# Expert blocks of a routed layer: the last 26 blocks with their three PE steps interleaved over three blocks, and separate places for the two weights

## Chip, core and metric

The kernel runs on one core of a Trainium2 chip. The metric is the device time of one launch in microseconds; times before are the median of three runs. One further execution was recorded by the profiler, and all engine times below come from it.

## What is computed

The reference is one layer over 6250 nodes with 256 features, all in float32:

```python
xn = layernorm(x)
x  = x + gnn(xn, edges) + linear_attention(xn)      # 100000 edges, sorted by target
z  = layernorm(x)
gate = z @ gate_w + gate_b                          # 16 experts, top 2 of them, softmax weights
h    = relu(z @ w1[e] + b1[e])                      # 256 -> 512
y    = h @ w2[e] + b2[e]                            # 512 -> 256
out  = x + layernorm(z + sum_over_top2(weight * y)) * gamma + beta
```

A graph part, a linear attention part and a mixture of experts follow each other for each node; the routing of a node can be computed as soon as its own row is done.

## The kernel before

Nodes are cut into 49 tiles of 128 rows. The host lays out one row of `experts` per expert and partition: the first product's weights (`WA` = 1024 floats), then the second product's weights with both biases (1284 floats). `WROW` is their sum.

Everything from the edge stage on is written as small Python generators that a `Weave` runs. A generator is added with a slot number, does a step, and yields how many slots later its next step comes; steps of one slot run in the order in which their generators were added. A slot is no time. It only fixes the order in which instructions are recorded, and so the order within each engine's queue and within SP's queue of DMA issues. Each engine then works through its own list in order and waits where data or a buffer isn't ready.

The stages in slot order:

- Edge stage: 782 chunks of 128 edges. For each, POOL gathers 128 rows (L1181), DVE builds a selection matrix (L1185), and PE multiplies six slots later (L1194). One chunk per slot.
- `residual(...)` finishes the rows of two tiles; `route(...)` assigns the tokens of a phase of tiles to slots of expert blocks of 128 tokens; `scatter(...)` sends the tokens to `xslots` (L931). `PHASES` lists the phase ends 8, 12, ..., 40, 46, 49. The last phase has `flush` true: it also closes all half filled blocks.
- `expert(n, j, ...)` is one block, 114 in all. With `s` its first slot and gaps (5, 4): at `s` SP issues the load of the first weights (called w1 here) and of the block's tokens x; at `s+5` the load of the second weights and both biases (w2); at `s+9` PE transposes x (`xtp`, L995) and ACT copies the result (L999); at `s+11` PE does the first product (`hp`, L1005) and ACT adds the bias and applies relu (L1010); at `s+13` PE does the second product (`yp`, L1014) and DVE adds the bias (L1018); at `s+15` SP issues the store to `yslots`. All DMA issues of a block go through the helper at L959. Blocks of phases up to the ninth start 7 slots apart, later ones 4 slots apart. Blocks 88 to 113 belong to the last phase.
- `combine(ts_, ...)` finishes a pair of tiles: POOL gathers the two expert rows of each token (L1044), ACT prepares the row (L1052), DVE adds the weighted rows (L1059), takes the statistics (L315, L316), gets the inverse deviation through ACT's square root (L321, L322) and normalises (L1067, L1068, L1070), then SP stores the output. The pairs of tiles 0 to 35 (`CUT` = 36) need only blocks up to number 84 and are added 5 slots apart beside the last blocks; the pairs of tiles 36 to 48 are added from 18 slots after the last block's start, and their gathers wait for the stores of all blocks.

Buffers are handed out by `Places`: `take()` gives the first free place in a list, `give()` puts it back at the end. A place made of tiles of `Q` can be taken only when those tiles have been read by the stage that wrote them. `homes["w"]` has four places of `WROW` floats: two in the tile `early` and two of ten tiles of `Q` each (14 to 23, 24 to 33). `x` has three places, `xT`, `hT` and `y` have two each, `got` (what combine gathers) has fourteen. The PSUM results of a block, `xtp`, `hp` and `yp`, come from one pool of six banks.

If the token counts were unusual, a second version behind a branch (L1214) would do all blocks again; with these inputs it is not run.

Of the kernel before, what the change touches and what calls it, by code (L numbers as in the profile page):

```python
# [31 lines left out]
P = 128  # L32
N = 6250
D = 256
# [17 lines left out]
FJ = F // P  # L52
KB = (2 * N + NE * (BLK - 1)) // BLK
WROW = 2 * F + FJ * D + FJ + D
# [72 lines left out]
WA = 2 * F  # L127
# [112 lines left out]
def windowed_layer(ctx: ExitStack, tc: tile.TileContext, X, rows3, ident, loc_t, w_t, W, b, gamma, beta, wqT, wkvT, wprojT, bproj,  # L240
# [6 lines left out]
    def bcast(ap, n):  # L247
        return bass.AP(tensor=ap.tensor, offset=ap.offset, ap=[[0, P], [1, n]])
# [88 lines left out]
    early = wp.tile([P, 2 * WROW], F32, name="early")  # L337
# [178 lines left out]
    def bank(name):  # L516
        return ps.tile([P, 512], F32, name=name, tag="bank")
# [440 lines left out]
    def sync(to, source):  # L958
        issued[0] = nc.sync.dma_start(to, source).ins  # L959
        return issued[0]  # L960

    stores = {}

    def expert(n, j, homes, bank, gap):

        def row(i):
            if not loaded.get(i):
                _, regs = nc.values_load_multi_w_load_instructions(
                    s["rows"][0:1, i, j:min(j // 8 * 8 + 8, ends[j])], engines=[mybir.EngineType.SP],
                    min_val=0, max_val=(MOST if i == 0 else NE - 1) * P,  # L970
                    skip_runtime_bounds_check_because="bounded by a minimum where it is computed")
                loaded[i] = list(regs)
            return loaded[i].pop(0)

        at, slots = row(1), row(0)
        wp_ = homes["w"].take()
        w = wp_()[:, :WROW]
        sync(w[:, :WA], experts[bass.ds(at, P), :WA])
        xp = homes["x"].take()
        xs = xp()  # L980
        i = sync(xs, xslots[bass.ds(slots, P), :])
        if n is not None:
            for m in range(n + 1, len(PHASES)):
                tc.declare_no_dep(i, group=f"tokens_{m}", reason="a full block takes no more tokens")
            tc.add_to_no_dep_group("loads", i)
        yield gap[0]
        sync(w[:, WA:], experts[bass.ds(at, P), WA:])
        w1 = w[:, :WA].rearrange("p (c f) -> p c f", c=2)
        w2 = w[:, WA:WA + FJ * D].rearrange("p (j d) -> p j d", j=FJ)
        b1 = w[:, WA + FJ * D:WA + FJ * D + FJ]  # L990
        b2 = w[:, WROW - D:]
        yield gap[1]
        tp = bank("xtp").rearrange("p (k c) -> p k c", k=4)
        for c in range(2):
            nc.tensor.transpose(tp[:, c, :], xs[:, c * P:(c + 1) * P], ident)  # L995
        homes["x"].give(xp)
        xTp = homes["xT"].take()
        xT = xTp().rearrange("p (k c) -> p k c", k=2)
        nc.scalar.copy(xT, tp[:, :2, :])  # L999
        yield 2  # L1000

        hp = bank("hp").rearrange("p (f c) -> p f c", f=FJ)
        for f in range(FJ):
            for c in range(2):
                nc.tensor.matmul(hp[:, f, :], w1[:, c, f * P:(f + 1) * P], xT[:, c, :], start=(c == 0), stop=(c == 1))  # L1005
        homes["xT"].give(xTp)
        hTp = homes["hT"].take()
        hT = hTp().rearrange("p (k c) -> p k c", k=FJ)
        for f in range(FJ):
            act(hT[:, f, :], hp[:, f, :], AF.Relu, bias=b1[:, f:f + 1], scale=1.0)  # L1010
        yield 2
        yp = bank("yp")
        for f in range(FJ):
            nc.tensor.matmul(yp[:, :D], hT[:, f, :], w2[:, f, :], start=(f == 0), stop=(f == FJ - 1))  # L1014
        homes["hT"].give(hTp)
        y_ = homes["y"].take()
        y = y_()
        v.tensor_add(y, yp[:, :D], b2)  # L1018
        homes["w"].give(wp_)
        yield 2  # L1020
        before_it = issued[0]
        i = sync(yslots[bass.ds(slots, P), :], y)
        if n is not None:
            tc.declare_no_dep(i, group="stores", reason="every block has rows of its own", keep=[before_it])
            tc.add_to_no_dep_group("stores", i)
            stores[j] = i
            if j >= FIRST:
                tc.declare_no_dep(i, group="gathers", reason="later blocks hold no token of the first tiles")
                tc.add_to_no_dep_group("late", i)
        homes["y"].give(y_)  # L1030
# [67 lines left out]
    def spare(t, n=1):  # L1098
        return range(t, t + n), lambda: Q[:, t:t + n, :].rearrange("p t c -> p (t c)")

    homes = {"token": Places(*[spare(t) for t in range(4)]),
             "x": Places(*[spare(t) for t in (4, 5, 6)]),
             "xT": Places(spare(7), spare(8)),
             "hT": Places(*[((), lambda j=j: hTs[j]) for j in range(2)]),
             "y": Places(spare(13), spare(34)),
             "w": Places(((), lambda: early[:, :WROW]), ((), lambda: early[:, WROW:]), spare(14, 10), spare(24, 10)),
             "got": Places(*[spare(t) for t in range(35, NT)])}


    weave = Weave()  # L1110
    PRE = 14
    at = -PRE
# [3 lines left out]
    at = int(at) + 6  # L1116
# [11 lines left out]
    block, ends, scattered = 0, {}, 0  # L1128
    a = lo = 0
    for n, b in enumerate(PHASES):  # L1130
        flush = b == NT
        for t0 in range(a, b, 2):
            t1 = min(b, t0 + 2)
            at = max(at, min(NCH, 16 * t1 + 4) + LAG + 3)
            weave.add(at, residual(range(t0, t1)))
            last_at = at
            for t in range(t0, t1):
                summed_at[t] = at + 3
                if t + RING < NT and t >= 4:
                    sum_from(t + RING)  # L1140
            at += 10
        hi = USUAL if flush else 2 * b - (9 if n < AFTER else -1 if n == AFTER else 4)
        ready = max(last_at + RES, scattered - 2)
        weave.add(ready, route(a, b, lo, hi, n == 0, n == AFTER, flush))
        if flush or n == AFTER:
            weave.add(ready + 6, token_weights(*((CUT, NT) if flush else (0, CUT))))
        slow = 0 if flush else 1
        weave.add(ready + 2, scatter(n, a, b, 9, "token" if slow else "got", slow))
        scattered = ready + 11 + 2 * (b - a) * slow
        ready += 14 + (2 * (b - a) * slow)  # L1150
        for j in range(lo, hi):
            ends[j] = hi
            block = max(block + (7 if n <= AFTER else 4), ready)
            weave.add(block, expert(n, j, homes, bank, (4, 3) if n < 3 else (5, 4)))
            if j == FIRST - 1:
                ready_a = block + 18
        lo, a = hi, b
# [7 lines left out]
    at = max(ready_a, last_at + RES)  # L1165
    for t0 in range(0, NT, 2):
        if t0 == CUT:
            at = max(at, block + 18)
        weave.add(at, combine(range(t0, min(NT, t0 + 2)), homes, mp, last))
        at += 5  # L1170
    hrow = rows3.rearrange("p a (i d) -> p (a i) d", d=D)
# [3 lines left out]
    while slot < NCH + LAG or weave.steps:  # L1175
        for t in range(NT * (slot + PRE) // PRE, NT * (slot + PRE + 1) // PRE if slot < 0 else 0):
            table(t)
        c = slot
# [8 lines left out]
        c = slot - LAG  # L1187
# [26 lines left out]
    with tc.If(again), ExitStack() as tail:  # L1214
        tail.enter_context(by_hand(tc))
        mp = tail.enter_context(tc.tile_pool(name="w_again", bufs=2))
        ps = tail.enter_context(tc.tile_pool(name="w_again_ps", bufs=8, space=bass.MemoryType.PSUM))
        last = mp.tile([P, 2, D], F32, name="last", bufs=1)
        nc.sync.dma_start(last[:, 0, :], bcast(f_gamma, D))
        nc.sync.dma_start(last[:, 1, :], bcast(f_beta, D))  # L1220

        def places(n, size, name):
            tiles = [mp.tile([P, size], F32, name=f"{name}{j}", bufs=1) for j in range(n)]
            return Places(*[((), lambda t=t: t) for t in tiles])

        homes = {"x": places(4, D, "x"), "xT": places(2, D, "xT"), "hT": places(2, F, "hT"),
                 "y": places(2, D, "y"), "w": places(4, WROW, "w"), "got": places(8, D, "got")}
        weave = Weave()
        block = 0
        loaded.clear()  # L1230
        stores.clear()
        row = bank("row")
        nc.tensor.matmul(row[0:1, :P], s["code"], ident, start=True, stop=True)
        listed(row, 0, MOST, True)
        for j in range(MOST):
            ends[j] = MOST
            weave.add(block, expert(None, j, homes, bank, (5, 4)))
            block += 4
        block += 18
        for t0 in range(0, NT, 2):  # L1240
            weave.add(block, combine(range(t0, min(NT, t0 + 2)), homes, mp, last))
            block += 6
        slot = 0
        while weave.steps:
            weave.run(slot)
            slot += 1
# [485 lines left out]
```

## Time and profile before

| what | value |
|---|---|
| three runs, us | 1525.33, 1528.05, 1530.75 (median 1528.05) |
| profiled execution: its own time, us | 1528.39 |
| profiled execution: span of the trace, us | 1526.6 |
| granted TensorE clock, mean over the span | 0.941 |
| edge chunks' last products | about 1226 us from the start of the span |
| scatter of the last phase's tokens | 1279 to 1288 us |
| last 26 blocks, first product of the first to last add | 1320.3 to 1463.7 us |
| loads of the first and of the second weights | 114 of 512 KB, 114 of 642 KB |

The profile's lines give a start time in microseconds from the start of the span, a duration, the engine, the line of the kernel, the operation, "output <- inputs", shapes and a count of merged instructions. In square brackets stands the engine's idle time just ahead and what ended it. One float32 matmul is two recorded instructions. In tables by stretch the columns are PE, PEld (weight load), DVE, ACT and POOL busy microseconds with instruction counts, then granted clock, DMA share and GB/s.

### The profile page before, as it was taken

Reading aid. Unit: us, or ns where it says so; the run is one execution under the profiler, and the core shown is the slowest. Engines: PE = TensorE matmul, PEld = TensorE weight load, DVE = VectorE, ACT = ScalarE, POOL = GpSimd, SP = SyncE. Lnnn points to the kernel's source line nnn. Section 1 sums busy time; section 2 is a strip of 40 time slices with the busy share of each in tenths; the row PEclk is TensorE's granted clock in tenths of the full one; section 3 lists DMA queues with packets and bytes.
Section 4 is the critical chain, followed back from the end, with each engine's and each line's share of the span. In section 5 each row is a group of like instructions: output and inputs, shape, how many; then the busy total and the mean of one; then the engine's idle time right before and its main releaser. Section 6 shows DMA issues by size and latency. Waiting matters only on the chain.

```text
span 1526.6 us, 24293 instructions
## 1 busy us (share of the span) xinstructions
PE 1252.2 (82%) x6930; PEld 981.7 (64%) x6930; DVE 921.1 (60%) x3262; ACT 509.3 (33%) x1353; POOL 967.0 (63%) x999
## 2 busy tenths in 40 slices
PE   4869999988867989898898998979899887877720
PEld 3836666666645768677776776767778766666620
DVE  8753444468875655657457574665655653388845
ACT  3653444433231323233233232322323243444320
POOL 1017777777777777777777777777777631565142
PEclk9999999999878989899999999999999999999975
DMA  9889933333337768778677877876778757899942
GB/s 274 273 257 379 376 107 101 103 98 114 102 114 236 231 218 276 244 260 279 221 260 242 272 266 227 277 238 227 242 274 265 251 185 275 310 376 378 327 128 69
DMA packets 176557, 357.04 MB, mean 234 GB/s; under 512 B 26643, under 2 KB 115656, under 8 KB 176406
## 3 DMA queue, kind: packets, MB, share of 16 engines
q1 hardware_dynamic: 128458, 226.32, 42.9%
q0 software_dynamic: 47712, 128.17, 26.9%
q8 instruction: 62, 1.02, 0.3%
q10 hardware_dynamic: 236, 0.80, 0.2%
q14 instruction: 89, 0.73, 0.2%
HBM read 280.82 MB, written 74.36 MB: 233 GB/s over the span
## 4 chain that ended last, share of the span: by engine, by line
PE 39%; DVE 19%; DMA 15%; issue 5%; ACT 3%; POOL 2%; SPq 0%; ACTq 0%; POOLq 0%; DVEq 0%
PE acc L1194 12%; DMA rows<-w_hs,src_t 9%; PE yp L1014 9%; PE hp L1005 7%; DMA w_xslots<-Q,slot_i 3%; PE hp L671 2%; DVE xn L1059 2%; DVE hot L1185 2%; PE kq L553 2%; DVE bnst L315 2%; PE mix L687 2%; DMA Q<-in_experts 1%; DMA early<-in_experts 1%; POOL w_xslots L931 1%; PE gl L714 1%
## 5 line engine op out<-in xcount | busy, mean ns | idle before, releaser
L1181 POOL DMA_INDIRECT rows<-w_hs,src_t x782 | 758.1, 969 | 333.0 <-issue 100.0
L1194 PE MATMUL acc<-rows,hot 128*128 128x256 f32 x1564 | 446.2, 401 | 73.4 <-DMA rows<-w_hs,src_t 61.3
L1194 PEld LDWEIGHTS acc<-rows,hot 128*128 128x128 f32 x1564 | 276.2, 197 | 149.4 <-issue 61.3
L1185 DVE TENSOR_SCALAR hot<-iota_g,loc_t,w_t 128x128 f32<-128x128 f32 x782 | 247.1, 359 | 14.5 <-PE acc L1194 13.7
L1044 POOL DMA_INDIRECT Q<-w_yslots,slot_i x98 | 99.8, 1019 | 113.4 <-DMA w_yslots<-Q 64.4
L1005 PE MATMUL hp<-Q,early 128*128 128x128 f32 x1136 | 143.8, 281 | 12.5 <-ACT Q L999 12.2
L1005 PEld LDWEIGHTS hp<-Q,early 128*128 128x128 f32 x1136 | 139.6, 196 | 21.4 <-ACT Q L999 18.4
L931 POOL DMA_INDIRECT w_xslots<-Q,slot_i x98 | 103.2, 1053 | 75.6 <-issue 66.8
L1014 PE MATMUL yp<-early,hT 128*128 128x256 f32 x568 | 140.1, 390 | 12.8 <-ACT hT L1010 12.8
L1010 ACT ACTIVATE hT<-hp,early 128x128 f32<-128x128 f32 x284 | 81.1, 368 | 146.5 <-PE hp L1005 103.9
L1014 PEld LDWEIGHTS yp<-early,hT 128*128 128x128 f32 x568 | 107.8, 193 | 32.8 <-ACT hT L1010 18.4
L999 ACT COPY Q<-xtp 128x256 f32<-128x256 f32 x114 | 42.1, 370 | 249.1 <-PE xtp L995 239.6
L1203 DVE SCALAR_TENSOR_TENSOR agg<-acc,dinv,agg 64x256 f32<-64x256 f32 x135 | 65.2, 483 | 72.5 <-PE acc L1194 68.5
L1018 DVE TENSOR_TENSOR Q<-yp,early 128x256 f32<-128x256 f32 x71 | 30.1, 424 | 122.6 <-PE yp L1014 122.6
L553 PE MATMUL kq<-early,xnT 128*128 128x512 f32 (+1 forms) x196 | 98.1, 624 | 4.4 <-ACT xnT L549 4.4
L559 DVE SCALAR_TENSOR_TENSOR row<-two_a,two_b 128x256 f32<-128x256 f32 (+1 forms) x49 | 21.0, 429 | 131.6 <-ACT two_b L557 131.6
L1005 PE MATMUL hp<-Q 128*128 128x128 f32 x688 | 88.2, 283 | 12.8 <-ACT Q L999 12.8
L1005 PEld LDWEIGHTS hp<-Q 128*128 128x128 f32 x688 | 84.0, 196 | 19.0 <-ACT Q L999 17.8
L1014 PE MATMUL yp<-Q,hT 128*128 128x256 f32 x344 | 85.2, 391 | 13.2 <-ACT hT L1010 13.2
L1010 ACT ACTIVATE hT<-hp,Q 128x128 f32<-128x128 f32 x172 | 49.1, 368 | 99.0 <-PE hp L1005 53.8
L1014 PEld LDWEIGHTS yp<-Q,hT 128*128 128x128 f32 x344 | 64.7, 193 | 25.8 <-ACT hT L1010 17.6
L321 ACT ACTIVATE sd<-mv,eps_t 128x2 f32<-128x2 f32 (+2 forms) x76 | 22.8, 300 | 152.7 <-DVE mv L316 148.7
(272 smaller groups left out, 1774.2 us busy)
## 6 DMA issues: line engine op xcount, KB each, us to landing
early<-in_experts SPq DMA_DIRECT2D x71, 642.0 KB
early<-in_experts SPq DMA_DIRECT2D x71, 512.0 KB
Q<-in_experts SPq DMA_DIRECT2D x43, 642.0 KB
Q<-in_experts SPq DMA_DIRECT2D x43, 512.0 KB
w_xslots<-zero_b SPq DMA_DIRECT2D x16, 1024.0 KB
w_yslots<-zero_b SPq DMA_DIRECT2D x16, 1024.0 KB
Q<-w_xslots SPq DMA_DIRECT2D x114, 128.0 KB
w_yslots<-Q SPq DMA_DIRECT2D x114, 128.0 KB
```

Source lines behind the costliest of these rows:

```text
L315: v.bn_stats(st[:r], src_tile)
L553: nc.tensor.matmul(kq[:r], xnT[:, k, :r], wkq[:, k, :], start=(k == 0), stop=(k == 1))
L931: i = nc.gpsimd.indirect_dma_start(out=xslots, out_offset=IndirectOffsetOnAxis(ap=slot_i[:r, t, k:k + 1], axis=0), in_=y[:r], in_offset=No ...
L999: nc.scalar.copy(xT, tp[:, :2, :])
L1005: nc.tensor.matmul(hp[:, f, :], w1[:, c, f * P:(f + 1) * P], xT[:, c, :], start=(c == 0), stop=(c == 1))
L1010: act(hT[:, f, :], hp[:, f, :], AF.Relu, bias=b1[:, f:f + 1], scale=1.0)
L1014: nc.tensor.matmul(yp[:, :D], hT[:, f, :], w2[:, f, :], start=(f == 0), stop=(f == FJ - 1))
L1044: g = nc.gpsimd.indirect_dma_start(out=got[i, k]()[:r], out_offset=None, in_=yslots, in_offset=IndirectOffsetOnAxis(ap=slot_i[:r, t, k:k + ...
L1181: nc.gpsimd.indirect_dma_start(out=hrows[c], out_offset=None, in_=hs, in_offset=IndirectOffsetOnAxis(ap=src_t[:, c:c + 1], axis=0))
L1185: v.tensor_scalar(hots[c], iota_g[:, group_of(c) % 2, :], loc_t[:, c:c + 1], w_t[:, c:c + 1], op0=OP.is_equal, op1=OP.mult)
L1194: nc.tensor.matmul(accs[g], hots.pop(c), hrows.pop(c), start=begin, stop=end)
L1203: v.scalar_tensor_tensor(agg(t)[p0:p1], acc[p0:p1, :], dinv[p0:p1, t:t + 1], agg(t)[p0:p1], op0=OP.mult, op1=OP.add)
```

## The change

`expert` gets a parameter `apart`, the slots from the transposes to the first product and from the first to the second. It is 5 for the blocks of the last phase and 2 for all others, as before. The steps of a last-phase block then lie at `s+9`, `s+14`, `s+19` and the store at `s+21`. The weights are taken as two buffers: `w1` at `s`, given back after the first product, and `w2` at `s+5`, given back after the bias add. `w1` has two places in `early` and two of four tiles of `Q`; `w2` has two in `early` and two of six tiles of `Q`. The pairs of tiles from 36 on are added from 24 slots after the last block's start. The branch that is not run is adapted.

```diff
-    def expert(n, j, homes, bank, gap):
+    def expert(n, j, homes, bank, gap, apart):
...
-        wp_ = homes["w"].take()
-        w = wp_()[:, :WROW]
-        sync(w[:, :WA], experts[bass.ds(at, P), :WA])
+        w1p = homes["w1"].take()
+        w1 = w1p()
+        sync(w1, experts[bass.ds(at, P), :WA])
+        w1 = w1.rearrange("p (c f) -> p c f", c=2)
...
         yield gap[0]
-        sync(w[:, WA:], experts[bass.ds(at, P), WA:])
...
+        w2p = homes["w2"].take()
+        w = w2p()[:, :WROW - WA]
+        sync(w, experts[bass.ds(at, P), WA:])
...
         nc.scalar.copy(xT, tp[:, :2, :])
-        yield 2
+        yield apart
...
         homes["xT"].give(xTp)
+        homes["w1"].give(w1p)
...
             act(hT[:, f, :], hp[:, f, :], AF.Relu, bias=b1[:, f:f + 1], scale=1.0)
-        yield 2
+        yield apart
...
         v.tensor_add(y, yp[:, :D], b2)
-        homes["w"].give(wp_)
+        homes["w2"].give(w2p)
...
-             "w": Places(((), lambda: early[:, :WROW]), ((), lambda: early[:, WROW:]), spare(14, 10), spare(24, 10)),
+             "w1": Places(((), lambda: early[:, :WA]), ((), lambda: early[:, WA:2 * WA]), spare(14, 4), spare(18, 4)),
+             "w2": Places(((), lambda: early[:, 2 * WA:WA + WROW]), ((), lambda: early[:, WA + WROW:]),
+                          spare(22, 6), spare(28, 6)),
...
-            weave.add(block, expert(n, j, homes, bank, (4, 3) if n < 3 else (5, 4)))
+            weave.add(block, expert(n, j, homes, bank, (4, 3) if n < 3 else (5, 4), 5 if flush else 2))
...
         if t0 == CUT:
-            at = max(at, block + 18)
+            at = max(at, block + 24)
```

More of the change, by code (lines that the diff above doesn't have):

```diff
@@ L986, in expert @@
         yield gap[0]
-        sync(w[:, WA:], experts[bass.ds(at, P), WA:])
[L988 to L991, printed above, removed]
+        w2p = homes["w2"].take()
+        w = w2p()[:, :WROW - WA]
+        sync(w, experts[bass.ds(at, P), WA:])
+        w2 = w[:, :FJ * D].rearrange("p (j d) -> p j d", j=FJ)
+        b1 = w[:, FJ * D:FJ * D + FJ]
+        b2 = w[:, WROW - WA - D:]
         yield gap[1]
@@ L1226, in windowed_layer @@
         homes = {"x": places(4, D, "x"), "xT": places(2, D, "xT"), "hT": places(2, F, "hT"),
-                 "y": places(2, D, "y"), "w": places(4, WROW, "w"), "got": places(8, D, "got")}
+                 "y": places(2, D, "y"), "w1": places(4, WA, "w1"), "w2": places(4, WROW - WA, "w2"), "got": places(8, D, "got")}
         weave = Weave()
@@ L1236, in windowed_layer @@
             ends[j] = MOST
-            weave.add(block, expert(None, j, homes, bank, (5, 4)))
+            weave.add(block, expert(None, j, homes, bank, (5, 4), 2))
             block += 4
```

## The prediction

> **What bounds the kernel now.** I began with the page's engine shares and its chain of waits:
>
> ```profile
> span 1526.6 us, 24293 instructions
> PE 1252.2 (82%) x6930; PEld 981.7 (64%) x6930; DVE 921.1 (60%) x3262; ACT 509.3 (33%) x1353; POOL 967.0 (63%) x999
> PE 39%; DVE 19%; DMA 15%; issue 5%; ACT 3%; POOL 2%; SPq 0%; ACTq 0%; POOLq 0%; DVEq 0%
> ```
>
> PE leads, but that averages stages. The edit's reordering concerns only the 26 blocks listed by the last routing (numbers 88 to 113; L761 writes 26 of them). The trace in order of time, PE alone, puts their first product at 1320.3 us and their last add at 1463.7. Three of its lines show one block's pattern:
>
> ```profile
> 1441.74 2.05 PE L1005 MATMUL hp<-Q,early 128*128 128x128 f32 x16 [0.52 <-ACT Q L999]
> 1444.30 1.99 PE L1014 MATMUL yp<-early,hT 128*128 128x256 f32 x8 [0.51 <-ACT hT L1010]
> 1446.13 0.38 PE L995 MATMUL xtp<-ident,Q 128*128 128x128 f32 x2
> ```
>
> hp waits for ACT's copy of the transposes, yp for ACT's relu, and nothing stands between. A period is 5.29 us (1288.61 to 1293.90). Where other products stand between, the chain gives hp 1.78 and yp 1.73; with 0.23 for the transposes the work is 3.74, so 1.55 us a block is waiting. That tempts one to 26 x 1.55 = 40 us. Busy time by stretch, with granted clock, DMA share and GB/s last, says no:
>
> ```profile
> 1386.00:1406.00 20.00, 15.79 (x100) 13.26 (x98) 18.00 (x51) 8.62 (x25) 11.86 (x13) 1.00 1.02 368
> 1406.00:1426.00 20.00, 15.25 (x90) 12.61 (x90) 18.56 (x53) 9.67 (x29) 9.23 (x9) 1.00 1.02 380
> 1440.00:1463.50 23.50, 18.06 (x109) 14.87 (x107) 7.02 (x19) 7.86 (x25) 0.00 (x0) 1.00 0.57 203
> ```
>
> In the first two, DVE (third figure) is 90 to 93% busy and the DMA share is full: the combine of tiles 0 to 35 runs there beside the blocks. DVE's waits from 1326 to 1440 confirm it:
>
> ```profile
> DVE rs L322 <- ACT sd L321: 5.5, 8, 1.5
> DVE Q L1018 <- PE yp L1014: 0.5, 1, 0.5
> ```
>
> PE costs DVE 0.5 us in 114. Only when combine's first 36 tiles are done, at 1445.9 (L1070 below), does PE set the pace:
>
> ```profile
> 1445.46 0.42 DVE L1070 TENSOR_TENSOR row<-xn,X 128x256 f32<-128x256 f32 x1
> 1446.33 0.42 DVE L1018 TENSOR_TENSOR Q<-yp,early 128x256 f32<-128x256 f32 x1 [0.45 <-PE yp L1014]
> 1452.73 0.42 DVE L1018 TENSOR_TENSOR Q<-yp,Q 128x256 f32<-128x256 f32 x1 [5.98 <-PE yp L1014]
> 1458.02 0.42 DVE L1018 TENSOR_TENSOR Q<-yp,early 128x256 f32<-128x256 f32 x1 [4.86 <-PE yp L1014]
> 1463.31 0.42 DVE L1018 TENSOR_TENSOR Q<-yp,Q 128x256 f32<-128x256 f32 x1 [4.86 <-PE yp L1014]
> ```
>
> These are the adds of blocks 110 to 113: 17.85 us from combine's pause to the last. Then the final store lets go the gathers of the last 13 tiles, whose DVE work fills the remaining 63 us.
>
> **The Trainium skill.** Perfetto Trace Analysis, "Identifying the Most-Contended Engine", says to judge TensorE's headroom otherwise than by matmul busy share, and VectorE by its occupancy; the windows agree: PE's 78% is a waiting PE, DVE's 93% a full one. DMA: Bandwidth & Descriptors, "Where 436 GB/s comes from", gives some 358 GB/s for memory to SBUF and 435 for the fabric. This trace moved 390 in 1366 to 1386, so the measurement decides: I use 375, the mean of the four 20 us stretches from 1346 to 1426 (362, 390, 368, 380). Its "Queues, rings and completion order" says that an engine serves its queues in turn, packet by packet; no view shows the turns, but SP's and POOL's queues took 80.0% and 19.9% of the engines from 1320 to 1440 side by side.
>
> **The change, part by part.** The instructions are the same before and after, loads and stores included; only order and places differ.
>
> 1. *PE order.* A block at slot s ran its steps at s+9 (transposes), s+11 (hp), s+13 (yp), s+15 (store); with apart = 5 they are s+9, s+14, s+19, s+21. With blocks 4 slots apart PE's order becomes xtp(b+2), hp(b+1), yp(b): each ACT step has about 2 us of other products to hide in. PE can save up to 40 us, but DVE hides all of it until combine pauses.
>
> 2. *DVE and ACT order.* The adds move 6 slots later relative to combine, so PE may be two blocks ahead when DVE comes to an add. At the pause four adds are left before (110 to 113) and five now (109 to 113). The first combine pair's square root leaves ACT before relu(88), not behind it. Before, relu ended at 1323.6, a table load of 1.28 followed and L1067 started at 1325.7; now the table load can follow the copy's end at 1320.3 and L1067 start near 1322.2. That is 3.5 us at DVE's head; I take 2.0, since the DMA is full just then (388 GB/s from 1320 to 1326), and keep 0 to 3.5.
>
> 3. *SP queue.* A w1 load stood behind the store of the block four earlier; that store now stands behind it, ahead of w2. Past it moves one 0.36 us issue and its wait for L1018. Between w2's issue and its add there were 8 slots and are 14, of 5.5/4 = 1.4 us each: 11 and 19 us, against landings of 6.3 to 7.9 in the chain. So ACT's waits for weights (10.0 us in five, 1326 to 1440) should nearly go. What is late next is DVE itself: I take 0 for them, range 0 to 3, as DVE hid most of them.
>
> 4. *Places.* w1 comes free after hp instead of after the add, about 2.9 us sooner; w2 as before. Ahead of block 88 this changes which buffer is used and no order. There POOL sets the pace (70 to 72 gathers per 100 us from 500 to 1100, 0.97 each beside 0.3 of issue) and the loads end under it: 0, bounded by -2 and +3 us, since w2 has only two places until tile 27 is read, where whole weights got a third at tile 23.
>
> 5. *The pause.* After its last output store SP has still to issue a store, w2(112), a store, w2(113): four issues at 0.57 make 2.3 us. 512 KB of w1(113) and twice 642 KB are then under way, 1.84 MB at 375 = 4.9 us; landing 5 us after issue puts w2(113) at 7.3. First relu 0.38, yp 2.0, add 0.42 make 10.1; with 0.4 of hand-overs 10.5. Bounds: 8.5 if the load lands in 3 us; 14.4 if PE is not ahead and does three hp (5.3) and five yp (8.7) after it, and an add. Gain 17.85 - 10.5 = 7.35.
>
> 6. *block + 24 for + 18* only keeps the last combines behind the later stores. POOL's order is unchanged, and they wait for the last store anyway: 0. The branch behind L1214 isn't run: 0.
>
> Sum: 7.35 + 2.0 = 9.35, say 9.4. Profiled execution 1528.39 (span 1526.6 and 1.8 around it) less 9.4 is 1519.0. The median shown is 0.34 lower, so 1518.7.
>
> **The rivals.**
>
> *Pause and head shrink (as summed).* Ends combined: 17.85 - 8.5 + 3.5 + 3 = 15.9, and 17.85 - 14.4 = 3.5 (the sum's middle is well above it). Chance 0.68.
>
> *The DMA takes it back.* From 1314.7 to 1463.5 some 50.4 MB moved. At 375 that is 134.5 us, so the last byte comes no earlier than 1449.2, and about 49.2 MB must come by the pause: 131.2 us, or 1445.9, with no idle engine; with the 3 us of idle that the stretches show, 1449. Then 10.5 ends at 1459.5, a gain of 4.2: 1523.9. For it: the full share. Against it: the lead of 19 us lets weights trail the pause. Chance 0.20.
>
> *PE sets the pace throughout.* 26 x 1.55 = 40: 1488. Against it: DVE's waits, and the DMA floor of 1449.2. Chance 0.03.
>
> *Slower: gathers starve.* With weights further ahead, SP's backlog delays POOL's gathers into the 14 got places, which are 3.5 pairs of 6.9 us ahead: 24 us. Beyond that landing each pair slips by (L - 24)/3.5; from L = 26 it eats the gain (18 x 0.57 = 10), and L = 28 gives 18 x 1.14 = 20.6 against 9.4: 1539. Against it: L1059 waited for gathers only in the last stage (6.9 us, three times), and queues served in turn. Chance 0.09 with lesser losses of this sign.
>
> That the order isn't what it says is excluded: PE's listing has it.
>
> **How the numbers follow.** This measurement can tell about 0.3% (4.6 us) from no change. Nearly all of the first case is faster (0.67); of the second 0.06 is faster and, with the rest of the first, 0.15 is within 0.3%; the third is faster, the fourth slower. So faster 0.76, same 0.15, slower 0.09. The range runs from the first case's far end to near no change: 1512.5 to 1526.0; the slower case and the third lie outside.
>
> **What would show it.** hp without a wait for ACT's copy; L1018 hardly waiting after the pause, and the last add some 10 us after combine's last L1070 instead of 17.85; the pause near 1444; stretches before it still 90% DVE at full DMA share; ACT's waits for weights near nothing; the end still 63 us behind the last add. Wrong would be: a pause before 1438, DVE waiting at L1059 for gathers, an end of the edge stage off 1226 by more than 3 us.

## The result, and the profile after

Five runs of the changed kernel gave a median of 1516.7 us (1514.49 to 1520.71), five of the kernel before 1528.11 us (1525.33 to 1531.29). The ratio is 0.9929, 95% interval 0.9907 to 0.9951: about 11 us faster. The profiled execution took 1519.05 us, 9.3 us less than that of before (1528.39). The forecast was 1519.0 for the profile and 1518.7 for the median, so the sum came out. Its parts did not: errors of up to 5 us cancelled, which is luck, and that is what the rest is about.

The page first: span, busy shares, and the shares of the chain of waits.

```profile
span 1517.3 us, 24250 instructions
PE 1245.4 (82%) x6930; PEld 982.9 (65%) x6930; DVE 919.5 (61%) x3262; ACT 505.6 (33%) x1353; POOL 968.8 (64%) x999
PE 39%; DVE 20%; DMA 14%; issue 6%; ACT 2%; POOL 2%; SPq 0%; ACTq 0%; POOLq 0%; DVEq 0%
```

At this height nothing has moved: the same work, the same shares. The difference has to be read by stage. The order is as the diff says; PE alone in the middle of the last blocks now shows transposes, first product and second product of three blocks in a row:

```profile
1392.96 0.38 PE L997 MATMUL xtp<-ident,Q 128*128 128x128 f32 x2
1393.18 1.95 PE L1007 MATMUL hp<-Q 128*128 128x128 f32 x16
1394.97 1.89 PE L1017 MATMUL yp<-early,hT 128*128 128x256 f32 x8
1397.93 0.41 PE L997 MATMUL xtp<-ident,Q 128*128 128x128 f32 x2 [1.06 <-DMA Q<-w_xslots]
```

Here hp and yp no longer wait for ACT. PE has its free time in one piece instead, ahead of the transposes. What ends it is in the waits from 1326 to 1440 (engine, line, what was waited for: us, times, longest):

```profile
PE xtp L997 <- DMA Q<-w_xslots: 21.0, 16, 2.5
DVE rs L322 <- ACT sd L321: 3.3, 9, 0.4
ACT hT L1013 <- DMA early<-in_experts: 1.6, 1, 1.6
```

The first line is new: the loads of the tokens x, which nothing waited for in the kernel before. The third shows that the waits for weights went, from 10.0 us to 1.6, as forecast. Busy time by stretch (PE, PEld, DVE, ACT, POOL, then granted clock, DMA share, GB/s), the last row being the tail behind combine's pause:

```profile
1366.00:1386.00 20.00, 16.61 (x110) 14.30 (x108) 18.54 (x52) 9.60 (x32) 12.44 (x13) 1.00 1.04 398
1386.00:1406.00 20.00, 14.96 (x92) 13.26 (x93) 18.50 (x53) 8.18 (x25) 12.08 (x13) 0.91 1.01 366
1439.50:1455.50 16.00, 13.09 (x84) 11.62 (x84) 2.17 (x8) 6.11 (x18) 0.00 (x0) 1.00 0.65 231
```

DVE is still 93% busy and the transfers are still full. At the head, DVE's first pair comes through without its long wait for the square root (0.36 us in place of 3.60). First the kernel before, then the kernel after:

```profile
1325.26 0.17 DVE L322 RECIPROCAL rs<-sd 128x2 f32<-128x2 f32 x1 [3.60 <-ACT sd L321]
1326.74 0.42 DVE L1070 TENSOR_TENSOR row<-xn,X 128x256 f32<-128x256 f32 x1
```

```profile
1321.72 0.17 DVE L322 RECIPROCAL rs<-sd 128x2 f32<-128x2 f32 x1 [0.36 <-ACT sd L321]
1322.85 0.42 DVE L1073 TENSOR_TENSOR row<-xn,X 128x256 f32<-128x256 f32 x1
```

And DVE at the end, from the last output row ahead of the pause to the last five adds:

```profile
1439.11 0.42 DVE L1073 TENSOR_TENSOR row<-xn,X 128x256 f32<-128x256 f32 x1
1440.65 0.42 DVE L1021 TENSOR_TENSOR Q<-yp,early 128x256 f32<-128x256 f32 x1 [1.11 <-DMA w_yslots<-Q]
1446.54 0.42 DVE L1021 TENSOR_TENSOR Q<-yp,Q 128x256 f32<-128x256 f32 x1 [5.46 <-PE hp L1007]
1449.82 0.42 DVE L1021 TENSOR_TENSOR Q<-yp,early 128x256 f32<-128x256 f32 x1 [2.86 <-PE yp L1017]
1453.34 0.42 DVE L1021 TENSOR_TENSOR Q<-yp,Q 128x256 f32<-128x256 f32 x1 [3.09 <-PE yp L1017]
1455.06 0.42 DVE L1021 TENSOR_TENSOR Q<-yp,early 128x256 f32<-128x256 f32 x1 [1.30 <-PE yp L1017]
```

With these marks the 9.3 us of span can be laid out. The first output row is marked by the start of its last DVE instruction, the pause by the end of that of tile 35. Each row is a difference of two times within each trace:

| stretch | before, us | after, us | gain | forecast |
|---|---|---|---|---|
| start to the first product of block 88 | 1320.34 | 1320.04 | 0.3 | 0 |
| from there to combine's first output row | 6.40 | 2.81 | 3.6 | 2.0 |
| first output row to the pause | 119.14 | 116.68 | 2.5 | 0 |
| pause to the last add | 17.85 | 15.95 | 1.9 | 7.35 |
| last add to the end | 62.87 | 61.82 | 1.05 | 0 |

The tail gave a quarter of what was expected; the head, the stretch with full transfers and a full DVE, and the end gave the rest. For that stretch, here is all of it, before and after (columns as above):

```profile
1326.74:1445.88 119.14, 92.48 (x565) 77.75 (x565) 107.03 (x295) 51.61 (x156) 58.29 (x58) 1.00 0.98 356
1322.85:1439.54 116.69, 89.50 (x570) 77.54 (x568) 107.00 (x295) 50.02 (x162) 60.77 (x60) 0.97 1.00 372
```

DVE is busy for the same 107.0 us in both. What shrank is its waiting: 6.0 us before (5.5 for the square root, 0.5 for an add), 3.3 us after.

### The profile page after: what moved, and what is told of

It is laid out like the page before. It is cut to its first block, busy times and chain, and to the rows that moved or that the text cites. A ratio compares the mean times of both kernels' runs of the same rounds, so it can differ in the third digit from the quotient of the medians.

```text
span 1517.3 us, 24250 instructions
## 1 busy us (share of the span) xinstructions
PE 1245.4 (82%) x6930; PEld 982.9 (65%) x6930; DVE 919.5 (61%) x3262; ACT 505.6 (33%) x1353; POOL 968.8 (64%) x999
## 3 DMA queue, kind: packets, MB, share of 16 engines
q8 instruction: 62, 1.02, 0.3%
## 4 chain that ended last, share of the span: by engine, by line
PE 39%; DVE 20%; DMA 14%; issue 6%; ACT 2%; POOL 2%; SPq 0%; ACTq 0%; POOLq 0%; DVEq 0%
PE acc L1199 12%; PE yp L1017 9%; DMA rows<-w_hs,src_t 9%; PE hp L1007 7%; PE hp L671 3%; DMA Q<-w_xslots 2%; DVE hot L1190 2%; DVE xn L1062 2%; PE mix L687 2%; PE kq L553 2%; DVE bnst L315 2%; DMA w_xslots<-Q,slot_i 1%; POOL w_xslots L931 1%; DVE agg L1208 1%; DVE Q L1021 1%
## 5 line engine op out<-in xcount | busy, mean ns | idle before, releaser
L1017 PE MATMUL yp<-early,hT 128*128 128x256 f32 x592 | 148.3, 396 | 5.8 <-ACT hT L1013 5.8
L1007 PE MATMUL hp<-Q,early 128*128 128x128 f32 x992 | 127.6, 284 | 6.1 <-ACT Q L1001 6.0
L1007 PEld LDWEIGHTS hp<-Q,early 128*128 128x128 f32 x992 | 124.6, 200 | 11.7 <-ACT Q L1001 9.1
L1017 PEld LDWEIGHTS yp<-early,hT 128*128 128x128 f32 x592 | 115.4, 198 | 25.2 <-ACT hT L1013 9.0
L1007 PE MATMUL hp<-Q 128*128 128x128 f32 x832 | 106.3, 283 | 5.1 <-ACT Q L1001 5.0
L1007 PEld LDWEIGHTS hp<-Q 128*128 128x128 f32 x832 | 103.6, 198 | 9.4 <-ACT Q L1001 7.4
L559 DVE SCALAR_TENSOR_TENSOR row<-two_a,two_b 128x256 f32<-128x256 f32 (+1 forms) x49 | 21.1, 430 | 130.9 <-ACT two_b L557 130.9
L1017 PE MATMUL yp<-Q,hT 128*128 128x256 f32 x320 | 78.6, 390 | 3.4 <-ACT hT L1013 3.4
L1017 PEld LDWEIGHTS yp<-Q,hT 128*128 128x128 f32 x320 | 60.4, 194 | 13.2 <-ACT hT L1013 5.2
L556 ACT ACTIVATE two_a<-kq 128x512 f32<-128x512 f32 (+1 forms) x49 | 29.3, 597 | 118.2 <-issue 93.3
```

## Experiments

All of them ran on other chips than the two profiles above. They ran in three groups, each on one chip (the places, the head start, the first run of the lighter kernel before, and the first run of the tokens early; the kernel after itself, the second runs of these two, and the lighter kernel after; the remaining four). On those chips the kernel before took 1801 to 1825 us in the median and not 1528, so each kernel is read as a ratio to the kernel before on the same chip, and its stretches as times within its own trace, which is of one execution. One kernel (the tokens early, below) ran in two groups and gave 0.9962 and 0.9909; nothing smaller than some 0.005 is read between groups. Within a group the intervals (95%) apply. The kernel after itself ran only in the second group.

### The places alone

```diff
-            weave.add(block, expert(..., 5 if flush else 2))
+            weave.add(block, expert(..., 2))
-            at = max(at, block + 24)
+            at = max(at, block + 18)
```

> The two weights in places of their own, but every block with steps 2 slots apart and the last combines at block + 18 as before. My theory: places alone are worth nothing, since PE still waits for ACT in each block and SP still has the store in front of w1: within 2 us of before (ratio 0.999 to 1.001), pause of combine (end of L1070 of tile 35) at 1445 to 1447, last add at 1463 to 1465. Rival: freeing w1 after the first product lets weights come sooner and takes away ACT's 10 us of waiting for them: 3 to 6 us faster.

Measured: 0.9993 (0.9971 to 1.0014). First output row to pause 121.1 us, pause to last add 18.0 (17.85 before), and DVE's waits for the adds there are those of the kernel before:

```profile
1744.14 0.42 DVE L1021 TENSOR_TENSOR Q<-yp,early 128x256 f32<-128x256 f32 x1 [6.11 <-PE yp L1017]
1754.71 0.42 DVE L1021 TENSOR_TENSOR Q<-yp,early 128x256 f32<-128x256 f32 x1 [4.86 <-PE yp L1017]
```

The places are worth nothing by themselves; the gain comes with the order. Whether the order needs the new places isn't shown: it wasn't run with the old ones.

### The head start alone

The kernel before, with combine two slots earlier, so that its first square root stands ahead of relu(88) on ACT:

```diff
-                ready_a = block + 18
+                ready_a = block + 16
```

> The kernel before, with all combine pairs of tiles 0 to 35 added 2 slots earlier (ready_a = block + 16), so that the first square root stands ahead of relu(88) on ACT as in the changed kernel; nothing else. Theory: DVE's head start of some 3.6 us appears (first L1067 near 1322 instead of 1325.7) and the pause comes 3 us earlier, but PE's chain of 26 periods of 5.3 us ends where it did: last add within 1.5 us of 1463.7, total 0 to 1.5 us faster. Rival: the head alone is worth its 3.6 us in the total, and the interleaving only its tail: 3 to 4 us faster.

Measured: 1.0025 (1.000 to 1.005). The head start is there, 2.7 us from block 88's first product to the first output row where the places alone have 6.6. It is handed back: 1.9 us up to the pause (123.0 beside 121.1), most of it in DVE's waits for the square root, and 1.5 in the tail (19.4 beside 18.0). From block 88's first product to the last add it took 145.1 us, the places alone 145.6, the kernel before 143.4. What stays is PE's chain. From the first product of block 88 to that of block 113 PE takes 138.4 us in the kernel before and 140.1 here, where 25 periods of 5.29 alone make 132.3. So in the old order PE's chain was nearly as long as DVE's work, though DVE's waits for adds (0.5 us in the kernel before) don't show it. In the kernel after PE takes 129.6 us for the same way.

### DVE lighter, in the old order and in the new

Both kernels without the two normalising DVE instructions (L1067 and L1068 before, L1070 and L1071 after) for tiles 0 to 35, 72 instructions and about 33 us of DVE. The kernel before ran so in two groups.

```diff
-            v.scalar_tensor_tensor(y[:r], y[:r], mv[:r, i, 0:1], last[:r, 0, :], ...)
-            v.scalar_tensor_tensor(y[:r], y[:r], rs[:r, i:i + 1], last[:r, 1, :], ...)
+            if t >= CUT:
+                v.scalar_tensor_tensor(y[:r], y[:r], mv[:r, i, 0:1], last[:r, 0, :], ...)
+                v.scalar_tensor_tensor(y[:r], y[:r], rs[:r, i:i + 1], last[:r, 1, :], ...)
```

> The kernel before, without the normalisation L1067 and L1068 of tiles 0 to 35 (left out of the computation): 36 x 0.97 = 35 us of DVE less. Theory that DVE and PE were both near their limit: PE's chain of 26 x 5.29 = 137.5 us stays, so only the 6 us by which the stretch was longer than that can go: 1 to 6 us faster, last add at 1458 to 1463, pause well before the last blocks are done. Rival, DVE alone was the limit: the pause and all behind it come earlier by most of the 35 us: over 15 us faster.

> The kernel before without L1067 and L1068 of tiles 0 to 35 (left out of the computation). PE's chain stays: 1 to 6 us faster than before. Rival, DVE alone was the limit: over 15 us faster. Third possibility: with DVE out of the way SP issues sooner and the DMA is the limit: within 1 us of before.

> The changed kernel without the same two DVE instructions of tiles 0 to 35 (left out of the computation), 35 us of DVE less. If DVE set the pace of the changed stretch, the end moves to the DMA's floor: last add at 1446 to 1451 instead of 1455.5, 4 to 9 us faster than the changed kernel. If the DMA set it already: the pause comes earlier but the last add stays, within 2 us of the changed kernel.

Measured: the kernel before became slower by it, 1.0087 (1.0063 to 1.0112) and 1.0089 (1.0055 to 1.0124), which none of the expectations had. The kernel after with the cut gave 0.9945 (0.9924 to 0.9967), beside 0.9917 for the kernel after itself in that group: no faster.

In the old order the first output row to the pause took 135.3 us where the places alone took 121.1. The trace of the lighter kernel's second run shows three holes of 3.3, 5.6 and 4.2 us on PE, each followed by a slow stretch; that of its first run has three alike (4.2, 5.8, 3.3). First ACT, then PE, then the stretches around one of them:

```profile
1658.98 1.14 ACT L1010 ACTIVATE hT<-hp,Q 128x128 f32<-128x128 f32 x4 [6.16 <-DMA w_yslots<-Q]
```

```profile
1659.40 3.78 PE L1014 MATMUL yp<-Q,hT 128*128 128x256 f32 x8 [5.64 <-ACT hT L1010]
1664.12 3.78 PE L1005 MATMUL hp<-Q,early 128*128 128x128 f32 x16 [0.52 <-ACT Q L999]
1668.42 1.99 PE L1014 MATMUL yp<-early,hT 128*128 128x256 f32 x8 [0.51 <-ACT hT L1010]
```

```profile
1655.00:1660.00 5.00, 0.60 (x2) 0.51 (x3) 1.09 (x3) 1.02 (x4) 2.28 (x3) 0.80 1.02 381
1660.00:1665.00 5.00, 4.48 (x14) 3.35 (x13) 1.13 (x5) 1.18 (x4) 0.00 (x0) 0.50 0.72 278
```

Relu waits 6.16 us for a transfer of SP's queue while the transfers are full (1.02, 381 GB/s); PE stands still for 5.64 us; then the granted clock is 0.50 and a second product takes 3.78 us instead of 1.99. Ahead of the hole POOL had issued eight gathers nearly end to end (1647.3 to 1657.9). My reading is that the lighter DVE freed their places sooner, and that these gathers held up the second product's weights, which have the shorter lead in the old order. No run took the gathers away in the old order, so it stays a reading. That the clock falls after such a hole is shown; the Trainium skill, "TensorE: Matmul & The Clock Gate", "Part 1: The HAM clock gate", says the same (half rate after an idle window of about 3.4 us). The traces show it behind shorter gaps too: in the kernel after the clock fell behind gaps of 2.05 and 1.86 us (last section).

In the new order the lighter DVE waits some 25 us for the adds, and the time is not shorter: the first output row to the pause took 115.5 us, with DVE busy 74 of it and the transfers full. Columns as above:

```profile
1604.00:1719.50 115.50, 93.19 (x571) 82.54 (x570) 73.88 (x227) 51.55 (x162) 54.66 (x55) 0.93 1.01 368
```

So DVE is not alone in holding that stretch. What else does is not settled: the DMA share is 1.01, but PE too had 22 us of waits there.

### Fewer gathers in the new order

The kernel after without the second gather of each tile for tiles 0 to 35:

```diff
             for k in range(2):
+                if k == 1 and t < CUT:
+                    got[i, 1] = got[i, 0]
+                    continue
                 got[i, k] = homes["got"].take()
```

> The kernel after without the second of the two gathers for the first 36 tiles: what the first gather fetched is used twice, so the arithmetic on DVE and all of PE's and ACT's work stay, but 36 gathers of 128 KB, 4.7 MB, are not moved. It asks what holds the stretch between the first output row and the pause in the kernel after, 116 us with the DMA engines busy all the time (1.00) and DVE busy 106 us of it. Theory (the transfers do): 4.7 MB at 372 GB/s is 12.6 us less of transfer; the stretch falls to DVE's own 107 to 110 us, and the total by 5 to 9 us under the kernel after. Rival (DVE does, and the head start of 3.6 us was gained there): the stretch stays at 115 to 116 us, and the total that of the kernel after to 1 us. Against the rival stands that 72 DVE instructions less brought nothing in the kernel after.

Measured: 0.9924 (0.9894 to 0.9953). The kernel after didn't run in this group, so the total can't decide here; the stretch from first output row to pause does, with 116.5 us where the kernel after had 116.7 and, in the second group, 116.5. The theory, that the transfers hold the stretch, failed: 4.7 MB less changed nothing.

```profile
1594.00:1710.50 116.50, 92.08 (x573) 79.80 (x571) 106.84 (x296) 49.60 (x162) 18.87 (x20) 0.96 0.94 324
```

The transfers have room now (0.94, 324 GB/s), and DVE is where it was, 106.84 us busy with 3.3 us of waits. The remaining 6 us are spread over its 296 instructions, 0.02 us each. That is DVE's floor in this stretch, 116 us, the short waits for the square root included. Taken with the run before, something else holds a length of 115.5 us when DVE is light; that it is the transfers is likely by their share there, but no run lightened both. In the new order every kernel with full DVE work that had no hole in this stretch lies at 116.5 to 117.4 us, with the old order at 119.1 to 123.0. This is where the 2.5 us of the table come from: the new order brings the stretch down to DVE's floor.

### The tokens early

The kernel after, with the x loads of the last 26 blocks eight slots sooner, in seven places:

```diff
-             "x": Places(*[spare(t) for t in (4, 5, 6)]),
+             "x": Places(*[spare(t) for t in (4, 5, 6, 9, 10, 11, 12)]),
...
-            weave.add(block, expert(...))
+            weave.add(block - (8 if flush else 0), expert(..., 8 if flush else 0))    # x here, w1 eight slots on
```

> The changed kernel, with the token loads x of blocks 88 to 113 issued 8 slots before their w1 loads, and seven places for x instead of three. Theory: after the change PE waits for x at xtp (21 us in 16 waits), which DVE hides until the pause and which then makes the tail 16 us; with x early the xtp waits go, the tail from pause to last add falls from 16.0 to 10 to 11 us, pause unchanged at 1438 to 1441: 5 us faster than the changed kernel, ratio to before 0.988 to 0.991. Rival: the weights w2(112) and w2(113), issued behind combine's last output store, set the tail: no more than 1.5 us from the changed kernel (ratio 0.992 to 0.994).

> The changed kernel itself, as the reference for the others of this group. If the chip gives the edge stage its usual pace (end near 1227 us): 0.991 to 0.995 of before. If the core is held up as in the group before (edge stage ending near 1490 us), the ratio may be nearer to 1, with 4 to 12 us gained in the last stretch.

> The changed kernel with the token loads of blocks 88 to 113 issued 8 slots earlier and seven places for x. As for the first run of it: tail from pause to last add 10 to 11 us instead of 16, pause unchanged, 5 us faster than the changed kernel. Rival, the last w2 loads set the tail: within 1.5 us of the changed kernel.

Measured: 0.9962 (0.9930 to 0.9995) in the first group; in the second 0.9909 (0.9883 to 0.9935), beside 0.9917 (0.9895 to 0.9939) for the kernel after. PE's waits for x are gone from the trace (21.6 us for the kernel after in that group), and the tail is 12.2 us in both groups, beside 15.1 to 16.0 in the traces that leave the x loads where the kernel after has them (itself in both its profiles, the lighter DVE, fewer gathers):

```profile
1730.44 0.43 DVE L1024 TENSOR_TENSOR Q<-yp,early 128x256 f32<-128x256 f32 x1 [1.58 <-DMA w_yslots<-Q]
1734.30 0.42 DVE L1024 TENSOR_TENSOR Q<-yp,Q 128x256 f32<-128x256 f32 x1 [3.44 <-DMA w_yslots<-Q]
1736.26 0.42 DVE L1024 TENSOR_TENSOR Q<-yp,early 128x256 f32<-128x256 f32 x1 [1.53 <-PE hp L1010]
1738.91 0.42 DVE L1024 TENSOR_TENSOR Q<-yp,Q 128x256 f32<-128x256 f32 x1 [2.23 <-PE yp L1020]
1740.64 0.42 DVE L1024 TENSOR_TENSOR Q<-yp,early 128x256 f32<-128x256 f32 x1 [1.30 <-PE yp L1020]
```

PE runs through this tail without a gap: at the pause it is in the first of three first and four second products, so 12 us is PE's own work. The late tokens cost 3 to 4 us of tail. The 5 us of total that I expected don't show; the two intervals of the second group overlap nearly whole.

### The tokens ahead of their block's first weights

```diff
+        xp = homes["x"].take()
+        i = sync(xs, xslots[...])
         w1p = homes["w1"].take()
         sync(w1, experts[bass.ds(at, P), :WA])
-        xp = homes["x"].take()
-        i = sync(xs, xslots[...])
```

> The kernel after with one order changed: each block's token load (128 KB) is issued on SP ahead of its first product's weights and not behind them. Theory (the token loads are the late item of the last blocks: PE waited 21.0 us in 16 waits for them in the kernel after, none of them in the kernel before): the load is issued some 1 us sooner and no longer queues behind half a megabyte of its own block (512 KB at 375 GB/s is 1.4 us), so the two waits of the tail (1.85 and 1.51 us) shrink to near nothing and the tail falls from 16 to 13 us; total 1 to 3 us under the kernel after. Rival (every load of the stretch only shares one rate of transfer, and what is sooner for the tokens is later for the weights): the waits go from the tokens to the weights, and the total is that of the kernel after to 1 us.

Measured: 0.9967 (0.9941 to 0.9992). PE's waits for x fell to 12.2 us in 11, the tail to 14.6, less than half of the fall that I expected; no gain over the kernel after can be read from it. That the waits would go over to the weights, as the rival had it, doesn't show either.

### The seven blocks behind the ninth routing interleaved too

```diff
-            weave.add(block, expert(..., 5 if flush else 2))
+            weave.add(block, expert(..., 5 if n > AFTER else 2))
...
-                ready_a = block + 18
+                ready_a = block + 24
```

> The kernel after with the interleaving also for the seven blocks behind the ninth routing (81 to 87); the gathers of the last stage may then start 6 slots later behind block 80, since the store of the last of these blocks is recorded later. Theory (PE's waits between a block's steps, 1.55 us a block, set the length wherever the loads keep up): 7 x 1.55 = 10.9 us less of PE waiting, of which the loads, already at 0.95 to 0.99 of the time there, leave 3 to 6 us; less up to 2 us by the later gathers. Total 1 to 5 us under the kernel after. Rival (the loads set the length of that stretch): nothing is gained, and the later gathers cost 0 to 3 us.

Measured: 0.9864 (0.9841 to 0.9888), the lowest ratio of the study, and below the swap of the same group (the tokens ahead of their weights, above) with the intervals well apart. Where that comes from is only in part shown, since the kernel after didn't run in this group and the swap has another order of loads. From the end of the edge stage to the last add it took 248.5 us, the swap 253.3, and 4.1 of these 4.7 us lie in the tail. PE comes to block 87 sooner, as the theory says (87.5 us behind the edge stage, the swap 101.8), but the first output row comes only 1.0 us sooner. Another 9 us between the two traces lie ahead of the end of the edge stage, where PE's order is still the same in both; no cause for these is shown. The tail is 10.55 us:

```profile
1703.71 0.42 DVE L1021 TENSOR_TENSOR Q<-yp,Q 128x256 f32<-128x256 f32 x1
1709.78 0.42 DVE L1021 TENSOR_TENSOR Q<-yp,early 128x256 f32<-128x256 f32 x1 [5.65 <-PE hp L1007]
1712.20 0.42 DVE L1021 TENSOR_TENSOR Q<-yp,Q 128x256 f32<-128x256 f32 x1 [1.99 <-PE yp L1017]
1713.92 0.42 DVE L1021 TENSOR_TENSOR Q<-yp,early 128x256 f32<-128x256 f32 x1 [1.30 <-PE yp L1017]
```

The edit has two parts, the interleaving and a start of combine that is recorded six slots later. My reading of the tail is the second: at the pause only three adds are left, and the last x load had landed by then. No run has one part without the other. The floor of 116 to 117 us in between is unchanged (117.4).

### Both together

The last two edits in one: the seven blocks interleaved, the tokens of the last 26 early.

> The kernel after with both: the seven blocks behind the ninth routing interleaved too (gathers 6 slots later), and the token loads of the last 26 blocks 8 slots ahead in seven places. Theory: the gain of the seven blocks (1 to 5 us) and the shorter tail (12.2 in place of 16 us), together 3 to 7 us under the kernel after, the fastest of all. Rival (the loads set the length up to the pause, and PE alone the tail): within 2 us of the kernel after.

Measured: 0.9888 (0.9848 to 0.9928, eight runs), faster than the kernel before, not told apart from the seven blocks alone, so not the fastest of all that I expected. The tail is down to 8.5 us. Its profiled execution lost 13.4 us on DVE in one wait behind the first output row:

```profile
1581.35 0.42 DVE L1024 TENSOR_TENSOR Q<-yp,early 128x256 f32<-128x256 f32 x1 [13.40 <-PE hp L1010]
```

In that hole PE issued single matmuls far apart (see the last section), so the 130.9 us from first row to pause aren't comparable; less the 13.4 they are 117.5, the floor again.

## Why the prediction was right, and where it was wrong

The total was right to 0.1 us in the profile and 2 us in the median. The mechanism stands in the main: the interleaving takes PE's waits for ACT away, nearly all of the 40 us this frees stays hidden behind DVE, and what is gained lies at the edges of that stretch and in DVE's short waits inside it. But that the sum came out is luck. The tail gave 5.45 us less than forecast; the head gave 1.6 more, the stretch 2.5, the end 1.05 and the start 0.3.

1. **PE order (point 1).** Right in the main. The waits of hp and yp went from 0.52 and 0.51 a block to next to nothing; PE's idle time went over to the transposes. That DVE hides all of it until the pause is too strong: the head start alone (1.0025) shows that in the old order PE's chain held the last add about as much as DVE did.

2. **Head (point 2).** Too small: 2.0 taken of a bound of 3.5, measured 3.6. I had marked it down because the transfers are full there. DVE had no wait for a gather there, so nothing held it back. Alone the head start is worth nothing; it counts because the new order lets PE follow, which point 2 did not say.

3. **Weights (point 3).** The waits went as forecast (10.0 to 1.6 us), and "what is late next is DVE itself" is right for this stretch. But I put the gain at 0 of 0 to 3, and it was 2.5. In the old order DVE lost those microseconds at the square root and at an add; in the new one the stretch is at DVE's floor of 116 us. The same point failed in what it left out: it followed the weights on SP's queue and not the third load of a block, the tokens.

4. **Places (point 4).** Right: 0 alone.

5. **The pause (point 5).** This is the step that failed: 10.5 us taken, bounds 8.5 to 14.4, measured 15.95. I took PE to be ahead at the pause and the landing of the last weights, w2(113), to be what the tail then waits for. Neither was so. At the pause PE still had three first and four second products to do, which is near the case of my upper bound; with the tokens early this work alone takes 12.2 us. And what PE waited for was no weight but x(112) and x(113). SP's queue, then PE:

```profile
1439.42 0.33 SPq L959 DMA_DIRECT2D Q<-w_xslots  x1
```

```profile
1440.43 0.41 PE L997 MATMUL xtp<-ident,Q 128*128 128x128 f32 x2 [1.85 <-DMA Q<-w_xslots]
1440.67 1.95 PE L1007 MATMUL hp<-Q,early 128*128 128x128 f32 x16
1442.46 1.89 PE L1017 MATMUL yp<-Q,hT 128*128 128x256 f32 x8
1445.86 0.41 PE L997 MATMUL xtp<-ident,Q 128*128 128x128 f32 x2 [1.51 <-DMA Q<-w_xslots]
1446.11 1.95 PE L1007 MATMUL hp<-Q,early 128*128 128x128 f32 x16
1447.89 1.89 PE L1017 MATMUL yp<-early,hT 128*128 128x256 f32 x8
1449.62 1.95 PE L1007 MATMUL hp<-Q 128*128 128x128 f32 x16
1451.41 1.89 PE L1017 MATMUL yp<-Q,hT 128*128 128x256 f32 x8
1453.14 1.89 PE L1017 MATMUL yp<-early,hT 128*128 128x256 f32 x8
```

The load of x(113) was issued at 1439.42, with the pause, and the chain of waits gives it 6.30 us to land. In the interleaved order the transposes of block 113 stand *ahead* of hp(112) and yp(111), and PE works in order: two first and three second products, 8.9 us with their hand-overs, and an add stand behind that one load. From the pause that makes 6.3 to the transposes, 0.25 for them, 8.9 and 0.5 for the add: 15.95. But PE worked through most of the 6.3 us; its idle time behind the pause is 0.9 us ahead of x(112) and 1.5 ahead of x(113). So of the 5.45 us by which the term was off the late tokens hold 3 to 4 (15.1 to 16.0 against 12.2), and the products that were still to do hold the rest. The weights held PE up nowhere in it: relu of block 113 waited for its first product and not for w2(113), though that load was issued 4.3 us behind the pause and not 2.3. A block's products moved 3 to 6 slots later relative to its weights, but the transposes did not move: x keeps its lead of 9 slots, and PE, no longer held up by ACT, now comes to it before it has landed (21.0 us of waits for x from 1326 to 1440, none in the kernel before).

6. **block + 24 and the end (point 6).** 0 was forecast; the end gained 1.05 us. The cause is open.

Of the rivals, "the DMA takes it back" named a possible limit with wrong numbers. It set the last byte needed by the pause at 1445.9 at best, with 375 GB/s and 49.2 MB. The pause came at 1439.5: the trace after moved 398 GB/s from 1340 to 1380, and only 46.9 MB from 1314 to 1439.5. The 398 are more than the 358 of the Trainium skill, "DMA: Bandwidth & Descriptors", "Where 436 GB/s comes from", which the page reckons as one core's half of what two cores share; this kernel runs on one core, and the measurement decides. A second limit near it exists, though: with a lighter DVE the stretch still took 115.5 us. "Gathers starve" did not happen, as DVE had no wait for gathers before the pause; "PE sets the pace throughout" did not either in the new order.

## What to carry to other kernels

When steps of several items are interleaved, list every load of an item with its lead over the step that reads it: the step that stays early becomes the late one, and in an in-order queue all later steps of older items stand behind it. Count, too, what the engine still has to do at the moment from which you reckon, before you take it to be waiting. Before forecasting what a lighter engine gives, work out each resource's own floor for the stretch, instruction gaps included; a second limit close behind makes the saving worth nothing. A total that comes out right says nothing about its terms until the two traces are compared at the same marks.

## What the runs showed of the hardware

- Less work made a kernel slower: 33 us less on DVE cost the old order 0.9%. Behind its hole of 5.6 us on PE the granted clock was 0.50; the second product (654 ns for one recorded matmul, 394 otherwise) and the first product after it both ran slow, until about 1668.
- The interleaved order brings a little of this, too. In the profile after the clock fell twice in the stretch, each time behind a gap ahead of the transposes (2.05 and 1.86 us); gaps of 2.48 and 2.07 us in the same trace had no such effect, and the stretch of the kernel before, with gaps of at most 1.45 us, has 1.00 throughout. DVE's floor seems to hide it. The first of the two:

```profile
1361.55 0.60 PE L997 MATMUL xtp<-ident,Q 128*128 128x128 f32 x2 [2.05 <-DVE bnst L315]
1361.94 3.43 PE L1007 MATMUL hp<-Q,early 128*128 128x128 f32 x16
```

- On the chips of the experiments PE stood nearly still for some 10 to 20 us around the start of combine, in every trace. In ten of them this lies ahead of block 88's first product, mostly as a wait for relu. In the two with the seven blocks interleaved it lies in the last 26 blocks: PE issued one matmul every 1.4 to 2.8 us and for the most part waited for nothing that the trace shows. The transfers sank as well (to 104 GB/s from 1575 to 1580 in the trace below). Here the kernel with the seven blocks:

```profile
1573.04 0.55 PE L1007 MATMUL hp<-Q 128*128 128x128 f32 x1 [1.05 <-issue]
1575.80 0.37 PE L1007 MATMUL hp<-Q 128*128 128x128 f32 x1 [2.22 <-issue]
```

The first two profiles, at the same place, have nothing of the kind. What causes it is open, and it is a part of what the totals of the experiments carry.
